# A two-layer graph kernel: the weights' product, the deviations, the fetch between two steps and the last sums rearranged

## The chip, the cores and the metric

The kernel runs on one core of a Trainium2 chip. The metric is the device time of one launch in microseconds; before the change it is 2241.94 us, the median of three runs between 2241.08 and 2243.65.

Names used below: PE is the matrix engine (TensorE), PEld its weight load, DVE the vector engine, ACT the scalar engine, POOL the GpSimd engine, SP the engine that issues most of the DMAs. L1074 means line 1074 of the kernel before.

## The reference

There are 3327 nodes with 256 features, padded to 26 tiles of 128 rows, and a weighted neighbour matrix `adj`. Two layers are applied. Cut to what matters:

```python
# layer 0, on h = relu(layernorm(x))
R = adj + I;  R = R / R.sum(-1)
for n in range(2):                                  # "step 1" and "step 2"
    q, k = Xa @ W1.T @ W2.T, Xa @ W3.T
    A = softmax(q @ k.T), largest entries kept until their sum is 0.9, rows rescaled
    Xf, Xa = R @ Xf, A @ Xa
    Z = Z + Xf @ U1[n].T + Xa @ U2[n].T
x = x + layernorm(h + Z) * ln_g + ln_b
# layer 1, on h = relu(layernorm(x)), 4 heads of 64
hp = h @ W                                          # s, d: two scores per node and head
e = leaky_relu(s_i + d_j) where adj_ij > 0
x = x + elu(softmax(e) @ hp)
```

Everything is float32.

## The kernel before

The function `fast` does the whole work. It doesn't issue instructions as it goes. It describes pieces to a planner, `Plan.put(engine, length, rank, fn, needs, take, give, lag)`: on which engine a piece runs, how long it should take, its rank (the smaller goes first when several are ready), the pieces it needs, the buffers that it takes and gives back, and after what lag its result is there. `Plan.order` plays these numbers through and gives one order for all pieces; `Plan.issue` then emits the instructions in that order. On the chip each engine works through its own queue in that order, and waits only for data and buffers. A piece whose function is `lambda: None` emits no instruction; it only moves other pieces in the plan. Since one order is made for everything, a changed length or need anywhere can move later pieces too.

The work runs in these stages.

- **Head.** `weights` (L689) loads all weights by eight DMAs on ACT's queue, and multiplies W1 by W2 into `wqk`: for each half of W1 a transpose (L703), a copy (L705), a product (L707) and two copies (L709), as one piece with rank -200. The 26 tiles of x are loaded by SP. `prepare` (L1108) then takes each tile through layer norm (`measure` on DVE, L676 and L678; `reciprocal_deviation` on POOL, L683 to L686, in a buffer `mv` of which there are four), relu (ACT, L1118), transposes (PE, L1123), a copy (DVE, L1126), the projection to keys and queries (PE, L1131), two copies on ACT (L1137, L1138), one on POOL (L1141) and a DMA that doubles the queries (L1144). `project_u` (L1163) makes the features' products with U1 and U2: one product (L1169) in a PSUM buffer `px` (there are two), a copy on ACT to `main` (L1172), and after it a copy on DVE to `c` (L1173).
- **Step 1 and step 2.** For each of 26 row tiles a `Row` computes logits against all keys (L856) and their exponents (L870), finds the threshold of the kept entries by counting on ACT (L907), a few steps on POOL (`step`) and sorting on DVE (L962 to L1017), then transposes the kept entries (L1030), copies them (L1035) and multiplies them by the features (L1042). `Full` multiplies the neighbour rows by the features (L1074): its tiles `at`, 256 KB each, are loaded by SP at L1063 into four buffers, and its sum is copied by ACT (L1081). In step 1 it multiplies `main`, in step 2 `c`.
- **Between the steps.** `finish1` makes the keys and queries of step 2 from each finished row. While step 1's last rows still read the old keys `kt` and queries `qq`, the new ones go to `kts` and `qqs` in memory. When the last row's logits are made, `fetch_keys` (L1253) brings the first 23 tiles back: two DMAs for the keys (L1257) and one for the queries (L1258). The last three tiles are written directly. All of step 2's `stats` (L781 and on) and `search` pieces need this fetch.
- **Layer 1.** `finish2` ends layer 0 for each row: it adds `late["b"]` to x (L1278) and stores the new x as `x1s` (L1294). `attend_neighbours` goes through 4 blocks of 832 columns: for each of 26 tiles masks on ACT (L1580, L1581), exponents on DVE (L1592), products (L1608) and denominators (L1622) on PE. At the end of a block the sums are copied (L1668, L1671), and for each of 7 pieces of 128 nodes: x1 is fetched (L1683) into a buffer `f`, the sums are turned (L1689), the denominator inverted (L1693), then ACT makes relu and exp head by head, 8 activations of 128x64 (L1701) into one of two buffers `ystage`, DVE adds in two instructions (L1705, L1706), and SP stores (L1709). After the last block a short check (`far`, `verdict`, L1797 to L1799) ends the kernel.

The fetch between the steps, as it stands:

```python
def fetch_keys():
    for r in range(2):
        ...
        nc.sync.dma_start(kt[half, :w], kts[half, :w])
    nc.sync.dma_start(qq[:, : LAST + 1, :], qqs[:, : LAST + 1, :])
```

Of the kernel before, what the change touches and what calls it, by code (L numbers as in the profile page):

```python
# [19 lines left out]
P = 128  # L20
# [5 lines left out]
H = 4  # L26
# [544 lines left out]
def fast(  # L571
# [59 lines left out]
    with ExitStack() as l0:  # L631
# [57 lines left out]
        def weights():  # L689
            w1 = etpool.tile([P, 4, P], F32, name="et")  # L690
            w1 = w1[:, 0, :].rearrange("p (c o) -> p c o", c=2)
            w2 = small.tile([P, PIECES, 8], F32, name="cands").rearrange("p c r -> p (c r)")[:DA, :DA]
            nc.scalar.dma_start(w1, w1t.rearrange("(c p) o -> p c o", p=P))
# [7 lines left out]
            for k in range(2):  # L701
                ps = ps_x.tile([DA, P], F32, name="px")
                T.transpose(ps, w1[:, k, :], ident)  # L703
                w1r = small.tile([P, P], F32, name="kq", bufs=BUFS["kq"])[:DA]
                S.copy(w1r, ps)  # L705
                ps = ps_x.tile([P, DA], F32, name="px")
                T.matmul(ps, w1r, w2, start=True, stop=True)  # L707
                for r in range(2):
                    S.copy(wqk[:, k, r, (1 - r) * DA : (2 - r) * DA], ps)  # L709
# [116 lines left out]
        plan = Plan(dict(rows=1, pl=2, px=2, acca=1, accf=1, accf0=1, accf1=1, et=3, at=4, y=1, e2=3, mask=2, **BUFS))  # L826
# [281 lines left out]
        def prepare(t, load):  # L1108
            mine, other, cols = half_of(t)
            held = {}  # L1110
            h = rhs[0][:, t, :]

            def first():
                held["mv"] = measure(h)

            def relu():
                mv = held["mv"]
                S.activation(h, h, AF.Relu, bias=mv[:, 3:4], scale=mv[:, 2:3])  # L1118
# [16 lines left out]
            def share():  # L1135
                held["kq"] = small.tile([P, P], F32, name="kq", bufs=BUFS["kq"])
                S.copy(held["kq"], held["ps"])  # L1137
                S.copy(qq[other, t, :], held["ps"][other])  # L1138

            def keys():  # L1140
                GP.tensor_copy(kt[mine, cols], held["kq"][mine])  # L1141

# [4 lines left out]
            a = plan.put("DVE", 0.62, r, first, needs=[load], take=["mv"])  # L1147
            a = plan.put("POOL", 1.1, r, lambda: reciprocal_deviation(held["mv"]), needs=[a])
            a = hs[0][t] = plan.put("ACT", 0.6, r, relu, needs=[a], give=["mv"])
# [3 lines left out]
            a = plan.put("ACT", 0.55, r, share, needs=[a], take=["kq"], give=["px"])  # L1153
            k = plan.put("POOL", 0.35, r, keys, needs=[a])
# [8 lines left out]
        def project_u(t, rank):  # L1163
# [9 lines left out]
            e = plan.put("DVE", 0.43, -2.6, lambda: V.tensor_copy(c[:, t, :], held["ps"][:, D:]), needs=[b], give=["px"])  # L1173
# [79 lines left out]
        def fetch_keys():  # L1253
            for r in range(2):
                half = slice(r * DA, r * DA + DA)
                w = max(half_of(t)[2].stop for t in range(LAST + 1) if side(t) == r)
                nc.sync.dma_start(kt[half, :w], kts[half, :w])  # L1257
            nc.sync.dma_start(qq[:, : LAST + 1, :], qqs[:, : LAST + 1, :])  # L1258
# [199 lines left out]
        def attend_neighbours(rows, ends, done, fulls):  # L1458
# [33 lines left out]
            def spread_heads(t0, t1):  # L1492
# [7 lines left out]
                def exps():  # L1500
                    held["rows"] = small.tile([7 * H, P], F32, name="rows", bufs=1)[: (t1 - t0) * H]
# [30 lines left out]

            used_heads = [None, None]
            evacuated = None
            both = broadcast(0, 59.5)
            for b in range(4):
# [140 lines left out]
                for x0 in range(0, W, P):  # L1677
# [25 lines left out]
                    def add(m=m, held=held):  # L1703
                        y = held["y"]
                        V.scalar_tensor_tensor(y[:m, 0], y[:m, 1], 1.0, y[:m, 0], ALU.min, ALU.add)  # L1705
                        V.scalar_tensor_tensor(y[:m, 0], y[:m, 0], -1.0, held["x1"][:m], ALU.add, ALU.add)  # L1706
# [5 lines left out]
                    f_ = plan.put("SP", 0.1, r1, fetch, needs=[touched, [a for a, _ in ends]], take=["f"], lag=3.0)  # L1712
                    a = plan.put(
                        "PE", 0.4, r1 + 0.02, turn, needs=[out_of], take=["px"], give=["e"] * (x0 + P >= W)
                    )
                    a = plan.put("DVE", 0.2, r1, invert, needs=[a], take=["mv"])
# [5 lines left out]
        LAST = NT - 4  # L1722

# [122 lines left out]
```

## Time and profile before

| what | before |
|---|---|
| median of 3 runs | 2241.94 us (2241.08 to 2243.65) |
| the profiled execution's own time | 2240.52 us |
| its span, first to last instruction | 2238.6 us |
| PE busy, 0 to 100 us | 81.6 us |
| PE busy, 800 to 900 us | 92.3 us |
| PE busy, 1100 to 1500 us | 397.2 us |
| PE busy, 1800 to 2200 us | 397.5 us |
| first reciprocal of the last block's end | 2217.08 us |
| last sum of the last block's end | ends at 2233.55 us |

The span is what the profiler sees between the first and the last instruction of one execution; the execution's own time lies 1.9 us above it, and the median of the runs 1.4 us above that. PE is nearly always busy between 100 and 2200 us, and clearly less so at the beginning, at the change from step 1 to step 2 (800 to 900 us) and at the very end. Busy times are sums over instructions; an engine that is busy can still be slow, when its clock is lowered, so the clock column is read beside them.

### The profile page before, as it was taken

Reading aid. Unit: us, or ns where it says so; the run is one execution under the profiler, and the core shown is the slowest. Engines: PE = TensorE matmul, PEld = TensorE weight load, DVE = VectorE, ACT = ScalarE, POOL = GpSimd, SP = SyncE. Lnnn points to the kernel's source line nnn. Section 1 sums busy time; section 2 is a strip of 40 time slices with the busy share of each in tenths; the row PEclk is TensorE's granted clock in tenths of the full one; section 3 lists DMA queues with packets and bytes.
Section 4 is the critical chain, followed back from the end, with each engine's and each line's share of the span. In section 5 each row is a group of like instructions: output and inputs, shape, how many; then the busy total and the mean of one; then the engine's idle time right before and its main releaser. Section 6 shows DMA issues by size and latency. Waiting matters only on the chain.

```text
span 2238.6 us, 36037 instructions
## 1 busy us (share of the span) xinstructions
PE 2177.3 (97%) x11978; PEld 1537.8 (69%) x11978; DVE 1615.0 (72%) x4229; ACT 1455.7 (65%) x2795; POOL 925.1 (41%) x2214
## 2 busy tenths in 40 slices
PE   7999999999999999999999999999999999999997
PEld 5487778777887778877878887887887433333332
DVE  5576657546655744178979877888777998989895
ACT  5776686566566652478887877878774455464653
POOL 6455355435544541256656666566653200000000
PEclk9999999999999999999999999999999999999998
DMA  3012221212212222621212222222225344444341
GB/s 99 20 38 70 68 70 54 70 49 64 70 53 70 70 83 67 191 76 56 76 49 70 59 74 72 81 62 66 69 75 154 121 129 137 116 144 119 102 128 42
DMA packets 192036, 183.76 MB, mean 82 GB/s; under 512 B 15354, under 2 KB 146144, under 8 KB 191712
## 3 DMA queue, kind: packets, MB, share of 16 engines
q1 hardware_dynamic: 189856, 180.10, 27.6%
q8 instruction: 96, 1.57, 0.3%
q10 hardware_dynamic: 1984, 1.26, 0.2%
q14 instruction: 100, 0.82, 0.1%
HBM read 164.41 MB, written 15.94 MB: 81 GB/s over the span
## 4 chain that ended last, share of the span: by engine, by line
PE 75%; ACT 8%; POOL 6%; DVE 5%; issue 3%; DMA 1%; SPq 0%; ACTq 0%; POOLq 0%; DVEq 0%
PE acca L1042 20%; PE accf L1074 20%; PE pl L1608 12%; PE px L1030 6%; PE pl L856 6%; ACT junk L907 5%; PE acca L1622 3%; PE accf L1622 3%; PE px L1217 2%; POOL sc L920 1%; PE px L1312 1%; PE px L1169 1%; DVE cands L967 1%; DVE y L962 1%; ACT et L1035 1%
## 5 line engine op out<-in xcount | busy, mean ns | idle before, releaser
L1042 PE MATMUL acca<-rhs,et 128*128 128x256 f32 x2704 | 619.4, 380 | 1.0 <-ACT et L1035 0.9
L907 ACT ACTIVATE junk<-e,sc 128x3327 fp8e5<-128x3327 f32 x182 | 559.2, 3073 | 48.1 <-POOL sc L952 46.8
L1042 PEld LDWEIGHTS acca<-rhs,et 128*128 128x128 f32 x2704 | 499.9, 191 | 64.4 <-ACT et L1035 2.9
L1074 PE MATMUL accf<-c,at 128*128 128x256 f32 x1352 | 313.5, 382 | 5.5 <-ACT f L1081 5.5
L1074 PE MATMUL accf<-main,at 128*128 128x257 f32 x1352 | 312.0, 382 | 5.6 <-DMA at<-in_adjt_dram 5.3
L962 DVE SCALAR_TENSOR_TENSOR y<-e,sc 128x1664 f32<-128x1664 f32 x104 | 209.0, 2010 | 149.0 <-POOL sc L949 147.0
L1074 PEld LDWEIGHTS accf<-main,at 128*128 128x128 f32 x1352 | 252.8, 191 | 47.9 <-issue 6.5
L1074 PEld LDWEIGHTS accf<-c,at 128*128 128x128 f32 x1352 | 250.0, 190 | 47.7 <-ACT f L1081 10.3
L1035 ACT COPY et<-px 128x512 f32<-128x512 f32 (+1 forms) x364 | 192.7, 553 | 136.1 <-PE acca L1042 72.9
L967 DVE MAX8 cands<-y 128x8 f32<-128x208 f32 x832 | 242.6, 361 | 3.6
L1017 DVE SCALAR_TENSOR_TENSOR e<-e,thr 128x832 f32<-128x832 f32 x208 | 213.1, 1082 | 2.2 <-DVE thr L1012 0.5
L870 ACT ACTIVATE e<-pl 128x1024 f32<-128x1024 f32 x208 | 179.0, 864 | 37.7 <-PE pl L856 37.5
L1581 ACT ACTIVATE et<-at 128x448 bf16<-128x448 f32 (+1 forms) x204 | 112.2, 550 | 137.3 <-DVE e L1592 81.5
L1030 PE MATMUL px<-ident,e 128*128 128x128 f32 x1352 | 191.2, 275 | 9.2 <-DVE gk L766 4.5
L1030 PEld LDWEIGHTS px<-ident,e 128*128 128x128 f32 x1352 | 159.5, 141 | 51.8 <-issue 15.3
L1608 PE MATMUL pl<-e,main 128*64 128x416 f32 x1024 | 187.2, 515 | 0.0
L856 PE MATMUL pl<-kt,qq 64*128 64x512 f32 (+1 forms) x832 | 173.5, 535 | 0.0
L1608 PEld LDWEIGHTS pl<-e,main 128*64 128x64 f32 x1024 | 71.0, 137 | 107.3 <-issue 92.0
L1592 DVE SCALAR_TENSOR_TENSOR e<-c,low,et 128x832 f32<-128x832 f32 x128 | 128.6, 1072 | 8.2 <-PE accf L1622 3.9
L856 PEld LDWEIGHTS pl<-kt,qq 64*128 64x128 f32 x832 | 71.6, 186 | 82.1 <-issue 75.7
L1592 DVE SCALAR_TENSOR_TENSOR e<-qq,low,et 128x832 f32<-128x832 f32 x120 | 120.5, 1074 | 2.6 <-ACT e L1668 2.0
L1580 ACT ACTIVATE at<-at 128x448 f32<-128x448 f32 (+1 forms) x204 | 109.8, 538 | 11.9 <-DMA at<-in_adjt_dram 11.8
(507 smaller groups left out, 2987.3 us busy)
## 6 DMA issues: line engine op xcount, KB each, us to landing
at<-in_adjt_dram SPq DMA_DIRECT2D x414, 256.0 KB
at<-in_adjt_dram SPq DMA_DIRECT2D x102, 192.0 KB
at<-in_adjt_dram SPq DMA_DIRECT2D x52, 128.0 KB
ys<-ystage SPq DMA_DIRECT2D x26, 256.0 KB
rhs<-in_x_dram SPq DMA_DIRECT2D x26, 128.0 KB
ystage<-in_x_dram SPq DMA_DIRECT2D x26, 128.0 KB
base<-ys SPq DMA_DIRECT2D x26, 128.0 KB
x1s<-ystage SPq DMA_DIRECT2D x26, 128.0 KB
```

The source lines that it names most:

```text
L856: T.matmul(pl[:, r, :m], qq[half, self.i, :], kt[half, 512 * k : 512 * k + m], start=True, stop=True,)
L870: S.activation(self.e[:, 1024 * k : 1024 * k + 2 * w].rearrange("p (r w) -> p r w", r=2), pl, AF.Exp, accum_out=(self.p0, self.p1, self.p2 ...
L907: S.activation(junk[:, :N], self.e[:, :N], fn, bias=t, scale=-1.0, accum_out=dst, saturate=False)
L962: V.scalar_tensor_tensor(self.y[:, : hi - lo], self.e[:, lo:hi], self.up, self.e[:, lo:hi], ALU.is_lt, ALU.mult, accum_out=(self.h0, self. ...
L967: V.max(self.cands[:, o // PIECE, :], self.y[:, o - lo : min(o + PIECE, hi) - lo])
L1017: V.scalar_tensor_tensor(piece, piece, self.thr[:, o : o + 1], piece, ALU.is_gt, ALU.mult)
L1030: T.transpose(pt[:, k, :], self.e[:, j * P : (j + 1) * P], ident)
L1035: S.copy(self.et[g][:, :m, :], self.pt.pop(g)[:, :m, :])
L1042: T.matmul(self.acc, et[:, j - 4 * g, :], rhs[self.n][:, j, :], start=(j == 0), stop=(j == NT - 1))
L1074: T.matmul(self.acc[:, : self.w], self.at[j // JC][:, j % JC, :], self.src[:, j, : self.w], start=(j == 0), stop=(j == NT - 1),)
L1592: V.scalar_tensor_tensor(held["e"][:, k, :], extra["both"][b % 2][:, k, :], low[:, j, k : k + 1], held["mask"], ALU.max, ALU.mult,)
L1608: T.matmul(q["acc"][a][k * FH : (k + 1) * FH, c, :C], main[:, j, h * FH : (h + 1) * FH], held["e"][:, h, c * C : (c + 1) * C], start=(j == 0),
```

## The change

It has five parts.

1. `weights` no longer is one piece. The DMAs are issued first; then four pieces follow: both transposes into one `px` tile (`turn`), two copies (`copy`), both products into one `px` tile (`product`), and two copies that place both halves at once (`place`). The first of them needs a piece on SP without instructions that ends after a planned 8 us.
2. The deviations of the head are made in groups of 1, 1, 2, 2, 2, 3, 3, 4, 4 and 4 tiles (`GROUPED`): DVE's statistics as before, but POOL's arithmetic once per group on several columns, in one of three buffers `mvs`. In `prepare`, the copy of the second half of the queries moves from ACT to POOL. In `project_u`, the copy to `c` needs the product alone, no longer the copy to `main`.
3. The fetch between the steps becomes five pieces: one for each half of the keys, three for the queries (tiles 0 to 7, 8 to 15, 16 to 22). Each needs the one before, with a planned lag of 5 us, through a POOL piece without instructions. Only the keys are needed by all rows of step 2; a row needs the queries' part that holds its own tile.
4. One is subtracted from `late["b"]` once, on POOL, so that `x1s` holds x1 - 1, and the -1 of elu is no longer added at the end. A constant does not change the layer norm that follows.
5. In the last block (`b == 3`) the end is shared by three engines: DVE divides all four heads at once (`quotient`), ACT makes relu and exp of 256 columns (`parts`), POOL adds x1 (`add_x1`), DVE joins (`join`). x1 is fetched for four pieces, then for three, into buffers that layer 1 no longer uses (`fetch_all`).

```diff
-            for k in range(2):
-                ps = ps_x.tile([DA, P], F32, name="px")
-                T.transpose(ps, w1[:, k, :], ident)
-                w1r = small.tile([P, P], F32, name="kq", bufs=BUFS["kq"])[:DA]
-                S.copy(w1r, ps)
-                ps = ps_x.tile([P, DA], F32, name="px")
-                T.matmul(ps, w1r, w2, start=True, stop=True)
...
+            a = plan.put("PE", 0.25, -200.0, turn, take=["px"], needs=[plan.put("SP", 0.02, -201.0, lambda: None, lag=8.0)])
+            a = plan.put("ACT", 0.5, -200.0, copy, needs=[a], take=["kq"], give=["px"])
+            a = plan.put("PE", 0.25, -200.0, product, needs=[a], take=["px"], give=["kq"])
+            return plan.put("ACT", 0.5, -200.0, place, needs=[a], give=["px"])
...
+            def rest():
+                mv = held["mv"][:, :m]
+                GP.tensor_scalar(mv[:, :, 2], mv[:, :, 1], LN_EPS, None, ALU.add)
+                GP.tensor_tensor(mv[:, :, 2], mv[:, :, 2], powers[:, 0:1].to_broadcast([P, m]), ALU.pow)
+                GP.tensor_tensor(mv[:, :, 3], mv[:, :, 0], mv[:, :, 2], ALU.mult)
+                GP.tensor_scalar(mv[:, :, 3], mv[:, :, 3], -1.0, None, ALU.mult)
...
-                S.copy(qq[other, t, :], held["ps"][other])
...
                 GP.tensor_copy(kt[mine, cols], held["kq"][mine])
+                GP.tensor_copy(qq[other, t, :], held["kq"][other])
...
-            e = plan.put("DVE", 0.43, -2.6, lambda: V.tensor_copy(c[:, t, :], held["ps"][:, D:]), needs=[b], give=["px"])
+            e = plan.put("DVE", 0.43, -2.6, lambda: V.tensor_copy(c[:, t, :], held["ps"][:, D:]), needs=[a])
+            plan.put("SP", 0.0, -2.6, lambda: None, needs=[b, e], give=["px"], lag=0.0)
...
+                for fn, args, rest in (
+                    (fetch_keys, (0,), ends[: LAST + 1]), (fetch_keys, (1,), ends[: LAST + 1]),
+                    *((fetch_queries, (lo, min(lo + 8, LAST + 1)), ends[lo : lo + 8]) for lo in range(0, LAST + 1, 8)),
+                ):
+                    p = plan.put("SP", 0.1, base + NT, fn, *args, needs=[after, [k for k, _, _ in rest]], lag=5.0)
...
+                    after = [plan.put("POOL", 0.02, -90.0, lambda: None, needs=[p], lag=0.0)]
...
+                    if b == 3:
+                        a = plan.put("DVE", 0.65, r1, quotient, needs=[a, f_], give=["px"])
+                        a = plan.put("ACT", 0.8, r1, parts, needs=[a])
+                        z_ = plan.put("POOL", 0.8, r1, add_x1, needs=[a, f_])
+                        a = plan.put("DVE", 0.45, r1, join, needs=[z_], hold=0.4)
+                        plan.put("SP", 0.1, r1, store, needs=[a], lag=2.5)
+                        continue
```

The four functions of the last block's end, without their slices:

```python
quotient:  V.reciprocal(rec, pr[:, 2, ::32]);  V.tensor_tensor(y[:, 1], pr[:, :2], rec broadcast, ALU.mult)
parts:     S.activation(y[:, 0], y[:, 1], AF.Relu);  S.activation(y[:, 1], y[:, 1], AF.Exp)
add_x1:    GP.tensor_add(y[:, 2], y[:, 2], y[:, 0])
join:      V.scalar_tensor_tensor(y[:, 0], y[:, 1], 1.0, y[:, 2], ALU.min, ALU.add)
```

## What the change was predicted to do

> **What bounds the kernel now.** I read the page first, then PE's busy time by stretch, then PE's waits in the poor stretches, then the timeline there.
>
> ```profile
> span 2238.6 us, 36037 instructions
> PE 2177.3 (97%) x11978; PEld 1537.8 (69%) x11978; DVE 1615.0 (72%) x4229; ACT 1455.7 (65%) x2795; POOL 925.1 (41%) x2214
> ```
>
> PE stands still for 61.3 us of the span. The diff takes no matrix product away, so it can only win from those 61 us and from time at half clock. Where they lie (columns: stretch, its length, busy us and count on PE, PEld, DVE, ACT, POOL, granted clock, DMA share, GB/s):
>
> ```profile
> 0.00:10.00 10.00, 0.88 (x3) 0.61 (x3) 2.71 (x9) 1.54 (x2) 6.18 (x33) 1.00 0.76 216
> 10.00:20.00 10.00, 8.62 (x31) 5.13 (x32) 4.68 (x19) 6.15 (x18) 4.78 (x15) 1.00 0.82 259
> ...
> 808.00:810.00 2.00, 0.21 (x1) 0.00 (x0) 1.97 (x7) 0.10 (x1) 1.70 (x3) 1.00 0.94 380
> 810.00:812.00 2.00, 0.00 (x0) 0.00 (x0) 1.97 (x5) 1.36 (x4) 0.00 (x0) 0.87 0.91 366
> 812.00:814.00 2.00, 0.45 (x1) 0.46 (x2) 1.97 (x6) 0.00 (x0) 0.73 (x2) 0.50 1.05 377
> 814.00:816.00 2.00, 2.00 (x6) 1.54 (x6) 0.34 (x2) 0.00 (x0) 0.00 (x0) 0.50 0.26 99
> ...
> 2220.00:2230.00 10.00, 3.41 (x13) 1.90 (x13) 4.26 (x14) 7.44 (x36) 0.00 (x0) 0.56 0.32 99
> ```
>
> Head: 18.4 us idle up to 100 us (10.5 of them before 20). Change from step 1 to step 2: one hole at 808 to 813.5, with DMA at 370 GB/s, and then half clock. Tail: 17 us of the last 29. All the rest, 100 to 800 and 900 to 2200, has 18.5 us together. PE's waits in the first 14 us, in 60 to 100 and in 800 to 820:
>
> ```profile
> PE px L707 <- ACT kq L705: 6.2, 2, 5.8
> ...
> PE px L1169 <- DVE c L1173: 3.7, 3, 1.8
> ...
> PE accf L1074 <- DMA at<-in_adjt_dram: 5.3, 1, 5.3
> ```
>
> And the timeline at the three places (start, duration, in brackets the idle time before):
>
> ```profile
> 7.91 1.28 ACT L705 ACT_TABLE_LOAD   x1 [7.91 <-DMA u<-in_u2t_dram]
> 11.84 1.58 ACT L1118 ACTIVATE rhs<-rhs,mv 128x256 f32<-128x256 f32 x3
> 12.75 0.22 POOL L683 TENSOR_SCALAR mv<-mv 128x1 f32<-128x1 f32 x1 [3.81 <-DVE mv L678]
> ...
> 804.09 0.52 SPq L1258 DMA_DIRECT2D qq<-qqs  x1
> 804.71 3.86 SPq L1063 DMA_DIRECT2D at<-in_adjt_dram  x4
> ...
> 2217.30 3.38 ACT L1701 ACTIVATE ystage<-px,mv 128x64 f32<-128x64 f32 x16 [0.16 <-DVE mv L1693]
> 2233.13 0.42 DVE L1706 SCALAR_TENSOR_TENSOR ystage<-ystage,f 63x256 f32<-63x256 f32 x1
> ```
>
> The reader is to see: ACT's first relu comes after the whole weights' product; the neighbours' loads stand behind the fetch of queries (1472 KB by the DMA view); the tail is one ACT chain.
>
> [...] after the 5.3 us hole the clock column reads 0.50, and 12 matmuls of L1074 take 5.21 us, where 4 take 0.87 in the chain of waits elsewhere (2.6 for 12). [...] 128x64 with a scale pointer takes 1.69/8 = 0.21 us in sequence here, 128x256 with two pointers 0.53. [...]
>
> **Part by part.** Sums are against the profiled execution, 2240.52 us with a span of 2238.6; the median shown is 2241.94, 1.42 above, and moves by the same amount.
>
> *Head, weights.* ACT is held by its own eight weight DMAs until 7.88 and by the table load until 9.19; both stay. Then the old order does two rounds of copy, product, two copies (9.21 to 11.96) and only then relu. The new order puts the product behind a planned 8 us. In that plan four relus are ready earlier, so I place ACT thus: relus of tiles 0 to 3 at 0.53 from 9.19 to 11.3; two copies of 0.26, 11.8; on PE two products of 0.69, 13.2; two copies of 0.16 to 0.33, 13.5 to 13.7. The first projection stood at 13.71: it does not move. What moves is that four tiles, not two, are turned by then[...]: 1.2 us of PE work falls into idle time[...].
>
> *Head, deviations.* POOL waited 3.81 us until 12.75, since a deviation buffer is freed by a relu. With relu 0 done by 9.8 the next group starts about 2.9 us sooner. POOL's work: before, 26 tiles of 1.34 (5.04 to 6.38: 0.22 + 0.57 + 0.27 and gaps) and a key copy of 0.36 with its gap, 44 us. After, ten groups of four instructions: 0.22, the power 0.57 + 0.158 per further column (0.87, 1.98, 2.46 us at 3, 10, 13 columns of L811), 0.19, 0.22, gaps 0.36: 15.6 + 2.5 = 18.1; and two copies per tile, 0.29 + 0.34 (L1205) + gaps, 19.5: 37.6 us. ACT loses one 0.26 copy a tile, 6.8 us. Keys so end up to 9 us sooner than 55, but PE was filling most of that wait with L1169. What it can get back is its waits in 14 to 60, 3.8 us, and in 60 to 100, 3.7 us; of the latter little, because ACT's 3.07 us counts (L907) hold the copy of main that DVE's copy of c no longer waits for, and px still waits for both. I take 1.3 of the 7.5. **Head: -3.0**; ends -0.5 (reordered px use eats it) and -8.
>
> *Transition.* One fetch of 736 KB keys and 1472 KB queries becomes five DMAs (352, 384, 512, 512, 448 KB). The POOL pieces between them emit nothing: only the order in SP's queue spaces them, with loads of `at` between. PE eats a 256 KB `at` in 8 matmuls, 1.73 us, and has four. A part takes 0.52 MB / 370 GB/s = 1.4 us, less than one `at`: the hole should close. It is worth 5.34 us idle plus 5.21 - 2.6 = 2.6 at half clock, 7.9. And it is on the path: ACT's copy of f (L1081) waited for this PE group until 818.79, and the counts of row 25 stand behind it in ACT's queue, with that row's keys and step 2's first statistics (PE at 898) after them. I leave 1.9 for small waits. **-6.0**; ends 0 and -8. Three more SP issues of 0.5 us are hidden: SP mostly waits for buffers there.
>
> *Layer 1's constant.* One POOL instruction on 128x256, 0.73 at most (L1278), before row 0's sum of step 2; POOL is half idle there: 0. Adding x1 in blocks 0 to 2 takes 0.42 either way.
>
> *Tail.* Before, 7 tiles x 8 activations x 0.21 = 11.8 us of ACT, and stalls of 1.2 us for stores and for the two ystage buffers; first reciprocal 2217.08, last sum 2233.55. After, per tile: DVE 0.17 + 0.42 (like L1323) + 0.42 = 1.05 with gaps, ACT two of 0.37 to 0.5, POOL 0.72 (L1225), PE 0.9 at half clock. Seven tiles at 1.0 to 1.1 are 7.3; after the last quotient come ACT 0.8, POOL 0.75, DVE 0.45, of which half a microsecond overlaps: the last sum at about 2217.1 + 9.4 = 2226.5. x1 is fetched ahead into buffers free since 2208. The end, 5.05 us after the last sum, stays. **-7.0**; ends -5 (activations at 0.55, the verdict's PE and DVE steps in between) and -8.5.
>
> *Reordering.* Every later piece is planned anew. 18.5 us idle in the steady stretches can move either way; I take 0, with 3 on both sides.
>
> Sum: -3 - 6 - 7 = -16: 2224.5 for the profiled execution, **2226 for the median**.
>
> **Rivals.**
> 1. All three carry to the end: 2226, own range 2220 to 2233. For it: PE at 99% between, so an earlier start is an earlier end. Chance 0.60.
> 2. The hole stays, since SP sends the parts back to back wherever `at` buffers are full, or each part makes its own hole: -10, 2232. For it: nothing in the queue forces the spacing. Against: `at` buffers come free every 1.73 us in this stretch. 0.18.
> 3. Only the tail wins; the head's gain is used up by row 0's search, which waits for ACT and POOL anyway, and the hole stays: -7, 2235. Its poorer end lies within the bound of no change. 0.12.
> 4. Slower: in SP's in-order queue a key or query part falls behind a load of `at` that waits for its buffer. Such waits last 18.4 us at 817, 25.8 at 867, 20.3 at 942. From the point that a needed part lands after 898, step 2's statistics are late; behind the wait at 942 it lands at 963, 65 us late. DVE is busy 170 of 200 us in step 2, so it can win about half back: +32, 2258. Against: five parts at 5 us planned spacing end near 835. 0.10.
>
> **How the numbers follow.** Faster by over 0.2% (4.5 us, what a measurement can tell here): 0.60 + 0.18 + 0.07 of rival 3 = 0.85. Within: 0.05, the rest of rival 3. Slower: 0.10. Range 2218 to 2237: from all three terms near their good ends to rival 3; outside lie rival 4, a little of rival 3 and the best corner of 1.
>
> **What would show it.** Right: first L1118 near 9.2; no wait of PE for `at` above 1 us and no clock of 0.5 near 800 to 820; last sum within 10 us of the first reciprocal. Wrong: PE's idle time between 100 and 2200 up by more than 5 us; a first logit of step 2 later, from the last attention of step 1 on, than the 29 us now (878.6 to 907.4); ACT at 1.1 us a tile in the tail.

## The result, and the profile after

The changed kernel takes 2221.14 us, the median of four runs between 2220.74 and 2222.8, against 2241.51 us for the kernel before (four runs, 2241.02 to 2243.65). The ratio is 0.9913, with a 95% interval of 0.9901 to 0.9925: it is faster by 20.4 us. The profiled execution of the changed kernel was the slowest of its four, 2222.80 us; against the 2240.52 us of the one before, the two traces differ by 17.7 us.

The page of the changed kernel has the same two lines as before:

```profile
span 2221.0 us, 35941 instructions
PE 2171.0 (98%) x11978; PEld 1535.2 (69%) x11978; DVE 1613.7 (73%) x4229; ACT 1442.5 (65%) x2725; POOL 931.3 (42%) x2210
```

PE has the same 11978 matmuls. It stands still for 50.0 us instead of 61.3, and its busy time fell by 6.3 us for the same work, while the mean granted clock rose from 0.994 to 0.998: both sources that the prediction named have paid.

To see where, both traces are cut at the same pieces of work: up to the fetch between the steps, the fetch and the hole behind it, all up to the end of the last block, and the tail. The columns are those of the prediction's first table of stretches. The kernel before:

```profile
0.00:802.50 802.50, 779.53 (x3887) 602.53 (x3888) 483.17 (x1472) 543.65 (x1030) 407.64 (x1036) 1.00 0.21 61
802.50:818.70 16.20, 10.86 (x42) 8.80 (x40) 8.18 (x18) 1.72 (x5) 7.09 (x16) 0.79 0.69 220
818.70:2216.40 1397.70, 1381.42 (x8031) 923.55 (x8029) 1116.02 (x2715) 897.92 (x1703) 510.36 (x1163) 1.00 0.32 93
2216.40:2238.60 22.20, 5.52 (x27) 2.92 (x23) 7.64 (x24) 12.39 (x58) 0.00 (x0) 0.61 0.20 63
```

The changed kernel, at the same cuts, and then finer at the head, at the fetch and in the tail:

```profile
0.00:797.68 797.68, 776.95 (x3886) 602.26 (x3887) 482.57 (x1472) 537.00 (x1002) 408.05 (x1025) 1.00 0.21 61
797.68:807.35 9.67, 8.56 (x42) 7.16 (x41) 6.04 (x13) 1.72 (x5) 6.37 (x14) 1.00 0.74 189
807.35:2204.95 1397.60, 1381.40 (x8031) 923.47 (x8029) 1117.78 (x2721) 898.10 (x1703) 510.75 (x1165) 1.00 0.33 95
2204.95:2221.00 16.05, 4.07 (x27) 2.33 (x23) 7.34 (x24) 5.68 (x16) 6.13 (x7) 0.76 0.18 59
...
802.00:804.00 2.00, 1.40 (x7) 0.88 (x5) 1.97 (x3) 0.00 (x0) 1.89 (x2) 1.00 1.00 198
804.00:806.00 2.00, 1.49 (x7) 1.33 (x8) 2.00 (x8) 0.84 (x3) 0.89 (x3) 1.00 1.11 345
```

The second figure of each row, the length, gives the account: the head -4.8, the fetch -6.5 (with 42 matmuls in 9.67 us, and the clock at 1.00 where it was 0.79), the 1400 us between -0.1, the tail -6.15 (ACT's 58 instructions became 16, and POOL has 7 where it had none). The sum is -17.6 us. In the last two rows PE still loses a little at the fetch, while DMA is as busy as before (shares of 1.00 and 1.11, where the hole had 0.91 to 1.05), but PE's clock stays at 1.00.

PE's waits in the changed kernel, in the first 14 us, from 60 to 130, and around the fetch (us in total, times, longest):

```profile
PE pl L1165 <- ACT rhs L1160: 10.8, 1, 10.8
...
PE px L1209 <- ACT main L1212: 2.4, 2, 1.5
PE px L1047 <- ACT main L1212: 1.6, 1, 1.6
PE px L1209 <- DVE c L1213: 1.2, 1, 1.2
...
PE accf L1091 <- DMA at<-in_adjt_dram: 1.1, 1, 1.1
```

PE's first wait is now for the first relu (L1160, before L1118), no longer for the copy of the weights; the wait for the neighbours' tile (L1091, before L1074) is 1.1 us instead of 5.3. The timeline of the changed kernel at the three places:

```profile
8.81 1.28 ACT L1160 ACT_TABLE_LOAD   x1 [8.81 <-DMA u<-in_u2t_dram]
10.11 2.08 ACT L1160 ACTIVATE rhs<-rhs,mvs 128x256 f32<-128x256 f32 x4
14.10 0.69 PE L717 MATMUL px<-cands,rest 64*128 64x64 f32 x2
...
803.81 0.46 SPq L1297 DMA_DIRECT2D kt<-kts  x1
806.54 1.20 SPq L1080 DMA_DIRECT2D at<-in_adjt_dram  x2
807.79 0.90 SPq L1300 DMA_DIRECT2D qq<-qqs  x2
826.91 0.58 SPq L1300 DMA_DIRECT2D qq<-qqs  x1
...
2205.60 0.18 DVE L1770 RECIPROCAL rows<-px 128x4 f32<-128x4 f32 x1 [11.87 <-PE px L1732]
2206.78 3.03 POOL L1784 TENSOR_TENSOR qq<-qq 128x256 f32<-128x256 f32 x4 [453.68 <-ACT qq L1780]
2212.32 1.26 DVE L1788 SCALAR_TENSOR_TENSOR e<-e 128x256 f32<-128x256 f32 x2 [0.62 <-POOL e L1784]
2213.51 0.27 DVE L1911 TENSOR_REDUCE verdict<-px 1x1 f32<-1x128 f32 x1
2213.81 0.15 DVE L1912 TENSOR_TENSOR again<-verdict 1x1 int32<-1x1 f32 x1
```

Head: four relus in a row, then the weights' products (L717), as planned; but the DMA hold of ACT ended at 8.81 us, where it was 7.91 in the trace before. Fetch: parts of the keys (L1297) and queries (L1300) with loads of neighbours (L1080) between them; two of the query parts are issued together at 807.79, so the planned 5 us between parts are not kept everywhere. Tail: from the first reciprocal to the last sum 8.0 us (before 16.5), but the last instructions are now those of the final check, `verdict` and `again`, in DVE's queue behind the joins.

### The profile page after: what moved, and what is told of

Read it like the earlier page. It is cut to its first block, busy times and chain, and to the rows that moved or that the text cites. A ratio compares the mean times of both kernels' runs of the same rounds, so it can differ in the third digit from the quotient of the medians.

```text
span 2221.0 us, 35941 instructions
## 1 busy us (share of the span) xinstructions
PE 2171.0 (98%) x11978; PEld 1535.2 (69%) x11978; DVE 1613.7 (73%) x4229; ACT 1442.5 (65%) x2725; POOL 931.3 (42%) x2210
## 4 chain that ended last, share of the span: by engine, by line
PE 71%; issue 9%; ACT 8%; POOL 5%; DVE 5%; DMA 2%; SPq 0%; ACTq 0%; DVEq 0%; POOLq 0%
PE acca L1059 20%; PE accf L1091 20%; PE pl L1651 9%; PE pl L873 6%; ACT junk L924 6%; PE px L1047 6%; PE acca L1665 2%; PE accf L1665 2%; PE px L1258 2%; PE px L1209 1%; PE px L1354 1%; POOL sc L937 1%; ACT et L1052 1%; DVE e L1635 1%; PE px L1236 1%
## 5 line engine op out<-in xcount | busy, mean ns | idle before, releaser
L1059 PE MATMUL acca<-rhs,et 128*128 128x256 f32 x2704 | 620.7, 380 | 1.7 <-ACT et L1052 1.6
L1059 PEld LDWEIGHTS acca<-rhs,et 128*128 128x128 f32 x2704 | 499.4, 191 | 66.0 <-ACT et L1052 4.8
L1091 PE MATMUL accf<-c,at 128*128 128x256 f32 x1352 | 313.5, 382 | 6.1 <-ACT f L1098 6.1
L1091 PE MATMUL accf<-main,at 128*128 128x257 f32 x1352 | 310.3, 381 | 3.0 <-DMA at<-in_adjt_dram 2.8
L1091 PEld LDWEIGHTS accf<-c,at 128*128 128x128 f32 x1352 | 250.0, 190 | 48.3 <-ACT f L1098 10.9
L1091 PEld LDWEIGHTS accf<-main,at 128*128 128x128 f32 x1352 | 251.0, 190 | 44.9 <-issue 6.5
```

The costliest lines, as they stand in the source:

```text
L1059: T.matmul(self.acc, et[:, j - 4 * g, :], rhs[self.n][:, j, :], start=(j == 0), stop=(j == NT - 1))
L1091: T.matmul(self.acc[:, : self.w], self.at[j // JC][:, j % JC, :], self.src[:, j, : self.w], start=(j == 0), stop=(j == NT - 1),)
```

## The experiments

The stretches used below run from landmark to landmark in the traces: "first product" is the first product with step 1's kept entries (L1042 before, L1059 after), counted from the start of ACT's table load, so that the load's own start does not count; "step 1" runs from there to step 2's first statistics; "tail" from the first turn of the last block's end to the end of the span.

| kernel | time, us | first product | step 1 | tail |
|---|---|---|---|---|
| before | 2240.52 (profiled) | 107.01 | 783.06 | 22.10 |
| after | 2222.80 (profiled) | 101.82 | 775.98 | 15.98 |
| weights alone | 2238.79 | 104.55 | 781.25 | 22.71 |
| groups alone | 2244.25 | 110.87 | 781.89 | 22.46 |
| copy order alone | 2243.29 | 107.03 | 784.29 | 22.32 |
| weights and groups, old copy order | 2241.68 | 106.95 | 784.01 | 22.23 |
| fetch alone | 2234.19 | 109.07 | 773.04 | 22.43 |
| tail alone | 2232.29 | 107.56 | 780.78 | 15.56 |
| after, check early | 2219.15 | 101.62 | 775.37 | 14.18 |
| before, check early | 2243.27 | 108.42 | 783.99 | 23.31 |
| after, sums first | 2217.07 | 101.95 | 771.29 | 15.59 |
| after, unspaced | 2224.01 | 102.73 | 776.31 | 15.66 |

Single times of the kernel before lay between 2237.07 and 2243.65 us over all runs, so for a kernel with a single time the stretches are compared, not the whole times. The kernels with the old head alone (before, fetch alone, tail alone, before with the check early) differ among each other too: from 107.01 to 109.07 us at the first product. The kernels with the old fetch take 780.78 to 784.29 us for step 1, those with the new one 771.29 to 776.31.

**One part of the change at a time.** The kernel before, with the weights' product in pieces and nothing else:

```diff
-        weighed = plan.put("PE", 3.0, -200.0, weights, lag=2.0)
+        weighed = weights()        # turn, copy, product, place as four pieces
```

> The kernel before with the weights' product in four pieces and nothing else of the change. With the whole change, the first product with the features (L1042 before) came at 110.6 us instead of 114.9, and stage by stage 4.8 of 17.6 us were won before 800 us. Theory: the weights in pieces only let relus and transposes start sooner; the deviations on POOL then hold the tiles up as before, so this part alone brings 1 to 2 us: first product with the features near 113.3, time near 2240. Rival: it brings the whole head's gain: near 110.6, time near 2237. Second rival: nothing, POOL decides: 114.9.

Measured: the first product comes 2.5 us sooner after the table load (104.55 against 107.01), a little more than the theory had. The relus of the first tiles do come before the weights' product. At a later mark this part alone is worth 4.7 us, which is nearer to the first rival; the head is taken up again below.

The kernel before, with grouped deviations and the query copy on POOL:

```diff
+            a = plan.put("POOL", 1.1 + 0.2 * m, -100.0 + lo, rest, needs=[a])
-            a = plan.put("POOL", 1.1, r, lambda: reciprocal_deviation(held["mv"]), needs=[a])
-                S.copy(qq[other, t, :], held["ps"][other])
+                GP.tensor_copy(qq[other, t, :], held["kq"][other])
```

> The kernel before with the deviations in groups and the query copy on POOL, the weights' product left in one piece. Theory: POOL's work per tile falls, the keys end some us sooner, and PE gets back part of its 3.8 us of waits between 14 and 60 us: 2 to 3 us, first product with the features near 112.3, time near 2239. Rival: nothing, since relu still begins after the weights' product at 11.8 us and PE fills the waits with other products: 114.9, time near 2241.5. Second rival: all 4.3 us.

Measured: 110.87, which is 3.9 us later than in the trace before and 1.8 later than the latest of the kernels with the old head; no theory had that. The keys were ready sooner, the first logits of row 0 at 53.21 us instead of 59.06, and yet the row's first product came later. In between this trace has one more wait of PE of 2.6 us (at 115.6, for a `px` that DVE's copy of `c` holds), and two pieces of half clock of 3.41 us each, at 25.9 and 118.0, which the trace before has not.

The fetch in five parts, alone:

```diff
-            nc.sync.dma_start(kt[half, :w], kts[half, :w])   # both halves, then
-        nc.sync.dma_start(qq[:, : LAST + 1, :], qqs[:, : LAST + 1, :])
+    fetch_keys(0); fetch_keys(1); fetch_queries(0, 8); (8, 16); (16, 23)   # as five pieces
```

> The kernel before with the five-part fetch alone. Theory: the hole of 5.3 us in PE and the half clock after it go, 1 us of waiting stays: 6.5 us less between the last key product of step 1 at 802.5 us and ACT's copy of f, and nothing elsewhere: time near 2235, no stretch at clock 0.50 near 810. Rival: the plan's other changes are needed as well, and the hole comes back at another load: near 2239 or above.

Measured: step 1 takes 10.0 us less. At the place of the old hole this kernel's table of stretches has

```profile
808.00:814.00 6.00, 5.94 (x34) 4.91 (x33) 5.89 (x13) 3.23 (x8) 2.50 (x4) 1.00 0.85 260
```

PE is busy for 5.94 of 6 us at full clock, and it has no wait for `at` between 790 and 820 at all. Of the 10.0 us not all are the fetch's: about 2 us are a piece of half clock near 869 that the trace before has and this one has not (see the last section).

The last block's end on three engines, alone:

```diff
+                    if b == 3:
+                        quotient (DVE), parts (ACT), add_x1 (POOL), join (DVE), store (SP)
+                        continue
```

> The kernel before with the last block's end on three engines and the constant subtracted once. Theory: the last sum comes 8.5 us sooner, but the program's end follows the check's last instruction (again, 7.1 us before the end in both kernels) and not the last sum, so the time falls by about 6.2 us, to 2235.5; the end stands 7.0 to 7.1 us after the check's last instruction. Rival: the end follows the last sum by 5.05 us as predicted: 8.5 us, 2233.

Measured: the tail takes 15.56 instead of 22.10 us, -6.5. The last sum ends at 2223.1, and `again` at 2223.48, 6.6 us before the end of the span (the theory had 7.0 to 7.1), so the 8.5 us that the last sum wins do not all arrive.

**What holds the end.** The final check is emitted after the planned pieces, so on DVE and PE it comes last in the order of the code. Here it becomes planned pieces of their own among the blocks of layer 1, as soon as its inputs are there:

```diff
-        plan.issue(tc)
-        V.tensor_reduce(far, ...)      # and on, to far, verdict, again
+        a = plan.put("DVE", 1.5, 75.0, far_away, needs=[failed, [z[0] for z in ends]])
+        # twice: lay (DVE), turn (PE), top (DVE); then again (DVE)
+        plan.issue(tc)
```

> The changed kernel with its final check (far and verdict, whose inputs are complete when layer 0 has ended) placed among the last layer's blocks instead of after them. Theory: the changed kernel's end follows the check's last instruction, which stands in DVE's queue behind the last sums, 7.1 us before the end; with the check early the end follows the last sum and its store, at most 5.05 us after it: span 2 to 4 us shorter, 2217 to 2219. Rival: the end follows the last sum anyway, the check only ended beside it: span 2221, within 0.5.

Measured on the changed kernel: the tail takes 14.18 instead of 15.98 us. The timeline of this kernel's last microseconds on DVE ends with

```profile
2209.86 1.60 DVE L1788 SCALAR_TENSOR_TENSOR e<-e 128x256 f32<-128x256 f32 x3
```

The last sum ends at 2211.46, and nothing follows it on DVE; the span ends 5.84 us later, where in the changed kernel it ends 7.4 us after the last sum. This is still 0.8 us more than the 5.05 of the kernel before; why, these runs do not show.

> The kernel before with the same early check. In it the last sum ended 5.05 us and the check 7.1 us before the end. Theory: both stood about equally late, the store of the last sum is the other limit: span within 0.7 of 2238.6. Rival: the check alone set the end before as well, so that the span falls by 1.5 us or more.

The same edit on the kernel before won nothing: the tail takes 23.31 us, 1.2 more, and the end comes 5.14 us after the last sum (5.05 before). The spread of the whole time was larger than this theory had allowed (2243.27 us, start and tail both later), but its question is answered: before, the last sum set the end, and the check, done by 2231.46, did not.

**The second hole.** Both kernels have another wait of PE of 2.1 us after the fetch (near 868 before, 857 after), for the sum of the keys `gk`. DVE does step 1's failure test, 15 instructions, just ahead of the last of these sums. Here the test is made to need the last sum:

```diff
-            failed.append(plan.put("DVE", 2.2, base + NT, failures, n, needs=[[a for a, _ in found]]))
             if n == 0:
                 ends = [finish1(r, done[r.i], base + r.i + 0.2) for r in rows]
+            failed.append(plan.put("DVE", 2.2, base + NT, failures, n,
+                needs=[[a for a, _ in found], [g for _, g, _ in ends] if n == 0 else None]))
```

> The changed kernel with the failure test of step 1 (15 small DVE instructions) ordered after the last sum of keys (gk), which frees a px buffer that PE waits for. Theory: the hole that is left at the change of steps, 2.1 us of waiting and 3.4 us at half clock after it, goes: 3 to 4 us, span near 2217.3. Rival: the test is needed by step 2's first pieces, so its delay comes back there: span 2220 to 2221.

Measured: step 1 takes 771.29 instead of 775.98 us, -4.7. The stretch in this kernel,

```profile
850.00:866.00 16.00, 16.00 (x86) 13.42 (x85) 5.47 (x22) 4.81 (x10) 1.78 (x2) 1.00 0.18 51
```

and in the changed kernel without the edit,

```profile
850.00:866.00 16.00, 13.92 (x70) 11.12 (x69) 7.48 (x23) 4.22 (x9) 1.79 (x2) 0.89 0.17 52
```

86 matmuls instead of 70 in the same 16 us: the hole (2.08 us of idle time) and the half clock behind it (0.89 over the stretch) are both gone. The other traces tell the two apart. With the hole and the half clock, step 1 takes 775.37 to 776.31 us (after, check early, unspaced); with the hole, but no half clock behind it, 773.04 (fetch alone) and 773.79 (the later loads below); without the hole 771.29 and 771.46 (all three together, below). The hole itself and the clock are worth some 2 us each.

**Splitting or spacing.** The changed kernel, without the piece that spaces the five parts in the plan:

```diff
-                    after = [plan.put("POOL", 0.02, -90.0, lambda: None, needs=[p], lag=0.0)]
```

> The changed kernel with the five parts of the fetch without the planned 5 us between them: the two key parts then stand directly one behind the other in SP's queue, and two query parts before them; no query or key part moves behind later loads. Theory: the splitting alone does a part, but 736 KB of keys in one piece before four neighbour loads, with 1 MB of queries close ahead, bring PE's wait for a load back from 1.1 us to 2 to 4: span 2222 to 2226. Rival: the spacing does nothing, what counts is that the queries need not all be there at once: span 2221, wait of PE near 1.

Measured: step 1 takes 776.31 us, 0.3 more than with spacing; PE's wait for `at` is 2.1 us instead of 1.1. The order in SP's queue is

```profile
774.88 0.90 SPq L1300 DMA_DIRECT2D qq<-qqs  x2
...
799.09 1.24 SPq L1297 DMA_DIRECT2D kt<-kts  x2
800.42 3.50 SPq L1080 DMA_DIRECT2D at<-in_adjt_dram  x4
...
828.02 0.58 SPq L1300 DMA_DIRECT2D qq<-qqs  x1
```

Two query parts now go 24 us ahead of the keys, and the third 28 us behind them: without the planned 5 us the five parts still don't stand together. So the planned spacing is worth about one microsecond of wait and hardly any time. What the kernels with a short wait have in common is that at most 736 KB stand directly ahead of the neighbours' loads, where the kernel before had 2208 KB (802.75 to 804.61). Five parts one directly behind the other, the case that rival 2 of the prediction feared, stood in no run.

**Where the head's gain comes from.** At the first product the weights alone gave 2.5 us, the groups alone took 1.8 to 3.9, and yet all together give 5.2. Left over is the small edit in `project_u`. Alone, and then everything else of the head without it:

```diff
-            e = plan.put("DVE", 0.43, -2.6, copy of c, needs=[b], give=["px"])
+            e = plan.put("DVE", 0.43, -2.6, copy of c, needs=[a])
+            plan.put("SP", 0.0, -2.6, lambda: None, needs=[b, e], give=["px"], lag=0.0)
```

> The kernel before with one edit: DVE's copy of c no longer waits for ACT's copy of main. From the moment ACT is free of its weight DMAs (the table load) to the first product with the features, the kernels with the old head took 107.0 to 109.1 us in the runs so far, those with the new head 101.6 to 102.7, with the weights' pieces alone 104.6. Theory: this copy frees px sooner and is the missing 2 to 3 us: 105 to 106. Rival: ACT's counts hold px as before, since the copy of main has to be done too: 107 to 109.

> The kernel before with the weights' pieces, the groups and the query copy on POOL, but with the old order of the two copies (main, then c). Alone, the weights' pieces gave 104.6 us on the stretch from the table load to the first product with the features, the groups 110.9. Theory: the groups only pay once relu no longer waits for the weights, so both together give most of the new head's 102: 102 to 103.5, and the copy's order little. Rival: the groups cost what they cost alone, 3 us, and the copy's order is what makes up for it: 106 to 108.

Measured: the first product comes at 107.03 us with the edit alone (107.01 before), at 106.95 with weights and groups without it, and with all three at 101.82, and 101.62 to 102.73 in the three other kernels of the table that have all of the head. That looks as if the copy order were worth 5 us, but only with the other edits. Two things in the traces forbid this reading. In the trace of the edit alone PE is idle for 1.7 us less from the table load to the first product (10.7 instead of 12.4), and a piece of half clock of 3.41 us, at 30.8, takes it back. And the first product is not the same mark everywhere: PE has done 405 matmul instructions before it in the kernel before and in the changed one, 401 with the weights or the groups alone, 413 with both and the old copy order.

A mark that all kernels reach with the same work (2875 matmul instructions) is the first product of the 17th row, the 833rd instruction of this line. PE's part of the line alone in three kernels, before, weights alone and after, up to this mark:

```profile
0.00:602.50 602.50, 189.38 (x833) 153.67 (x834) 1.00 0.22 62
0.00:598.20 598.20, 190.28 (x833) 153.29 (x834) 1.00 0.22 62
0.00:597.70 597.70, 190.42 (x833) 153.28 (x834) 1.00 0.22 62
```

From the table load on, and with the half clock that lies before it:

| kernel | first product of the 17th row, us | half clock before it, us |
|---|---|---|
| old head (before, fetch alone, tail alone, before with the check early) | 594.6 to 595.9 | 0 |
| copy order alone | 595.4 | 3.4 |
| weights alone | 589.9 | 0 |
| groups alone | 597.1 | 6.8 |
| weights and groups, old copy order | 597.8 | 6.8 |
| whole new head (after, check early, sums first, unspaced) | 588.3 to 589.2 | 0 |

So the weights' pieces alone bring 4.7 us against the trace before, of the 5.7 that the whole head brings. The groups cost time, alone and beside the weights, and half clock is part of that cost. The copy order makes up for it, and all three together are 0.7 to 1.6 us better than the weights alone. This is the rival of the second of these two expectations in its main point: the groups cost what they cost alone, and the copy's order makes up for it. Weights and copy order without the groups were not run, so whether the groups are of any use stays open. PE's waits from 60 to 130 us in the kernel without it:

```profile
PE px L1209 <- DVE c L1213: 5.3, 4, 1.8
PE px L1047 <- ACT et L1052: 2.8, 1, 2.8
```

Without the edit, the product with U (L1209) waits for DVE's copy of `c` four times, 5.3 us, as the kernel before and the one with the weights alone do; with it 1.2 us remain, and 2.4 for the copy of `main`. What the groups add to the waits is the second line, and another of 3.0 us for `et` at 141.9, each with a piece of half clock at its end. A likely reading is that ACT, busy with row 0's counts (3.07 us each), comes late to its copies when the keys are early; the runs show the size and not this cause.

**A later load of U1 and U2.** ACT waits for its own eight weight DMAs, until 8.81 us in the changed kernel's trace, before it does anything else. U1 and U2 are not needed until the first features' product, so here SP loads them, U1 after eight tiles of x and U2 after all of them:

```diff
-                nc.scalar.dma_start(u1[:, :, cols], ...); nc.scalar.dma_start(u2[:, :, cols], ...)
+                for u, ut, r in ((u1, u1t, -192.5), (u2, u2t, -200.0 + NT)):
+                    plan.put("SP", 0.58, r, load_u)
```

> The changed kernel with the four 256 KB loads of U1 and U2 taken from ACT's queue and issued by SP, U1 after eight tiles of x and U2 after all. In the changed kernel ACT is held by its own DMAs until 7.7 to 8.8 us. Theory: that hold sets the start; the table load then comes near 3.2, the first relu near 5.4, and the first product with the features 2 to 4 us sooner: 106 to 108 against 109.4 to 111.4 us, span 2216 to 2219. It also takes the run-to-run spread of the start away. Rival: the weights' DMAs land no sooner and PE's first idle time only moves behind the table load: no gain.

Measured: the table load starts at 3.35 instead of 8.81 us, and PE's transposes at 5.75. But the first product comes at 111.32 us from the span's start (110.63 without the edit), the 17th row's at 597.96 (597.68), and the whole takes 2223.1 us: nothing gained. From 21 us on this kernel's table of stretches,

```profile
21.00:24.00 3.00, 3.00 (x14) 3.00 (x15) 0.82 (x4) 1.59 (x6) 1.91 (x7) 0.50 0.10 22
```

shows PE at half clock; in the 3 us before, it was busy for 1.39. The half clock is not what eats the gain: the next kernel has the same loads and none in the head, and reaches the 17th row at 596.63, where kernels with the old loads had 596.08 and 596.39. Where the start no longer limits, the statistics, relus and copies of 26 tiles and row 0's search still do; which of them, these runs leave open.

**All three together**, the check early, the sums first and the later loads:

> The changed kernel with the early check, the last sum of keys ahead of the failure test, and the later U loads together. Theory: the three act at different places of the path and add: 1.8 + 4.4 + 3, a median near 2212 and at least 8 us below the changed kernel's 2221.1. Rival: the new plan loses some of it elsewhere: 2214 to 2219.

Measured: 2216.14 us (2215.99 to 2217.35, four runs) against 2240.64 for the kernel before (seven runs on that chip), a ratio of 0.9895 with an interval of 0.9878 to 0.9911. The theory's 2212 was missed, since the later loads bring nothing, and the rival's 2214 to 2219 came. It is 24.5 us below the kernel before, where the change is 20.4 below it; the medians of the two lie 5.0 us apart and their traces 6.8, so that this does not settle whether the 6.5 us that the check and the sums gave one by one arrive in full.

## Why the prediction was right, and where it was not

The prediction's likeliest case came about: all three parts carry to the end. 2226 us was forecast, 2221 measured; against its own base, the profiled execution, it had 2224.5, and 2222.8 was measured.

**Base.** The prediction moved from the profiled execution to the median by one constant, 1.4 us. In the changed kernel the profiled run was 1.7 us above its own median, and the one before 1.0 below the median of its four runs. This is why the medians differ by 20.4 and the traces by 17.7. ACT's hold ended late in the changed kernel's trace, at 8.81 us; that this made it slow is likely, but not shown.

**Head: -3.0 forecast, -4.8 between the traces**, or -5.2 from the table load on. The sum came out near, but its terms did not. The weights' pieces were put at 1.7 us: 1.2 for two more tiles turned ahead of the first projection, at the 0.59 us a tile took in the trace before (four transposes in 1.18 us at 12.51), and 0.5 that was the author's estimate and that no trace had shown. The words with it were "The first projection stood at 13.71: it does not move"; alone the pieces bring 4.7 by the 17th row. The first projection indeed came no sooner (14.54), but the first logits did, at 53.95 us instead of 59.06, and PE's idle time from the table load to the 17th row's first product fell from 15.5 to 10.6 us. Which of PE's waits this was, no run takes apart. The 1.3 us that the groups and the other small edits were to get back are, on top of the weights, 0.7 to 1.6; but the groups by themselves cost time, though they brought the keys forward as forecast (first logits at 48.69 us in the changed kernel), and "of the latter little", said of the copy of `c`, was wrong beside the groups: the kernel without that edit is some 9 us later at the 17th row, and half clock is part of it. That the wrong sizes left a head of the forecast's order was luck. "First L1118 near 9.2" was missed by the DMA hold (10.11); the first projection, held to stay at 13.7, came at 16.05 in the changed kernel, behind the transposes of four tiles in PE's queue.

**Transition: -6.0 forecast, -6.5 measured.** The mechanism is as described: the wait for `at` fell from 5.3 to 1.1 us, and the clock reads 1.00 from 802 to 810. The limit "above 1 us" was just missed. The reason given for it, loads of `at` between the parts in SP's queue, held for most of them: two query parts were issued back to back, but behind such loads. Without the planned spacing the plan still kept the parts apart, and the time is nearly the same. Rival 2 did not come; that a hole would stay if all parts stood together was not tried. That the earlier start is passed on is shown by the middle row: 1397.60 against 1397.70 us.

**Tail: -7.0 forecast, -6.15 measured.** The sum up to the last sum was too cautious: 8.0 us from the first reciprocal where 9.4 were taken. Its own terms, 7.3 + 0.8 + 0.75 + 0.45 less 0.5, add up to 8.8, not 9.4. Activations took 0.40 to 0.42 us (0.37 to 0.5 was an estimate; in the trace before, ACT's copies of 128x257, L1081, took 0.37 and its relus of 128x256 0.53 in sequence), and POOL's additions 0.71 to 0.88, but for one of 1.65. What failed is the sentence "The end, 5.05 us after the last sum, stays". It had been the last sum's own distance; once the sums came 8.5 us sooner, the check's second reduction, whose transpose was done by 2210.69, stood in DVE's queue behind the joins until 2213.51, and the end follows `again` by 7.04 us (7.14 before). The rows of the early check show both sides of this: 1.8 us on the changed kernel, none before. The check is not all of it: with the check out of the way the end still comes 5.84 us after the last sum, not 5.05. The prediction had named "the verdict's PE and DVE steps in between" as a bound of this term, but did not take it.

**The rest.** The reordering was taken as 0 and gave -0.1 over 1400 us. The constant of layer 1 cost nothing that the trace shows. Rival 3 falls with the fetch and the head. Rival 4 needed a part landing after 898; the last was issued at 826.91, and the first statistics of step 2 came at 886.6. In small it did happen: this last part stood behind a load of `at` that was issued only at 824.10, 15 us after the part before, and there was time enough. Its price rested on a misread line: "18.4 us at 817, 25.8 at 867, 20.3 at 942" are merged rows of several loads, and the longest single waits in them are 16.4, 19.0 and 6.6 us. Of the signs of being wrong none came: PE's idle time between 100 and 2200 us fell from 26.2 to 21.3 us, and the first logit of step 2 follows the end of step 1's last attention by 22.62 us in both traces.

**Not seen.** The prediction said of the transition that one hole was to be had. The second one, 50 us later, was in the trace before too, as a wait of 2.1 us for `gk`, and was worth 4.7 us with the half clock behind it.

## What to carry to other kernels

When a transfer starves the matrix engine, split it and keep the parts apart in the queue, so that the loads behind get a turn: here PE's wait for `at` fell from 5.3 to 1.1 us, and to 2.1 without the planned spacing, so exact spacing mattered little. When a tail is shortened, look at what else stands in the same engines' queues at the end: an instruction ready for microseconds, but emitted last, can become the end, as the check's second reduction did here (its input was there by 2210.69, and it ran at 2213.51). And compare kernels at a mark that all reach with the same work: at the first product the weights' pieces seemed worth 2.5 us and the copy order 5, and at the 17th row nearly all of the gain was the weights'.

## What the hardware showed beside this

**Half clock came in pieces of 3.41 us, and a hole brought one when about 1.9 us of it lay in one window of that length.** The second hole was 2.1 us long in the kernel before and in the kernel with weights and groups but the old copy order. Just behind it the kernel before shows

```profile
870.00:872.00 2.00, 2.00 (x6) 1.64 (x6) 0.00 (x0) 0.58 (x1) 0.00 (x0) 0.50 0.00 0
```

and the other kernel, behind the same hole,

```profile
872.00:874.00 2.00, 2.00 (x13) 1.74 (x11) 0.00 (x0) 0.58 (x1) 0.00 (x0) 1.00 0.00 0
```

6 matmuls in 2 us at 0.50, 13 at 1.00. The same holds near 1710, where a wait of 1.9 us brought a clock of 0.66 over 5 us in the kernel with the fetch alone and a wait of 1.8 us none in the changed kernel; from step 2's first statistics to layer 1's first product (L1608 before) the first takes 833.1 us and the second 830.7.

Before the last block's end every piece of half clock in these traces is 3.41 or 6.83 us long, and within a trace the pieces start whole multiples of 3.413 us apart. In the trace before they start at 811.49, 869.52 and 2221.19 us, which is 17 and 396 times 3.413 us apart; in that of the copy order alone at 30.76, 812.41, 870.44, 1720.36 and 2225.53 us, which is 229, 17, 249 and 148 times.

Windows of 3.413 us, laid from these pieces over all 14 traces, number 8728 that lie between 60 and 2195 us and begin at full clock. After the 21 in which PE was idle for more than 1.93 us, half clock always followed; after the 8703 with at most 1.84 us, never; after the four between (1.86 to 1.91), once. In the trace before, the idle times that half clock followed are 3.28 and 2.09 us (windows from 808.08 and 866.10), and no other window that began at full clock has more than 1.71; in the changed kernel's it is 2.08 us (from 854.92), and no other has more than 1.77. So in these traces some 1.9 us of idle time were enough, if they lay in one window. The hole of the kernel before, 867.2 to 869.3, lies in the window that ends at 869.5. That of the other kernel, 869.6 to 871.7, is cut by a window's edge at 871.5 and leaves 1.86 us in the first. In the first 60 us and in the tail 1.1 to 1.7 us were enough five times, which this count does not explain. The edges lie elsewhere in each trace (from the span's start, 2.5 us behind a multiple of 3.413 us in the trace before and 1.6 us in the changed kernel's), so a difference of some 2 us in one stretch of a single trace is no evidence.

**The start varies by itself.** ACT's hold by its eight weight DMAs ended between 7.37 and 8.81 us in kernels that issue the same DMAs in the same order. How much of that reaches the end, the runs do not show.
